# Summing the values of two key tiles in one visit of TensorE, in a transformer layer on one core

## The chip, the cores and the metric

The program runs on one core of one Trainium2 chip, in one launch. The metric is the device time of one execution in microseconds, the median of several runs. A profile of one execution stands beside it, with every instruction's start and length by engine: PE (TensorE), ACT (ScalarE), DVE (VectorE), POOL (GpSimd), and SP, which issues the DMAs.

## The reference

The input is 8 sequences of 1024 tokens of 256 channels, in float32. Four parts follow one another, each added to the running value after a layer norm:

```python
x = x + retention(layernorm(x), ...)     # 4 heads, chunks, gates: "attn_a"
x = x + ffn(layernorm(x), ...)
x = x + attention(layernorm(x), ...)     # 16 heads of 16 channels: "attn_b"
x = x + ffn(layernorm(x), ...)           # the same weights again
```

What the change touches is the attention:

```python
scores = jnp.einsum('bhqd,bhkd->bhqk', q, k) / np.sqrt(HEAD_DIM)
attn = jax.nn.softmax(scores + bias[None], axis=-1)
out = jnp.einsum('bhqk,bhkd->bhqd', attn, v)
```

The bias depends on the distance of key and query alone, and is the same for all distances over 128.

## The kernel before, in words

**One planner for all.** The kernel's functions only record operations, each with a target time. `Plan.issue` then emits them in an order of its own: it keeps a clock by estimated costs, and whenever an engine is free it takes, among the operations of that engine that are ready and whose tiles find a buffer, the one of the smallest key. The key is the target plus surcharges. So the work of several sequences is mixed on each engine: retention and feed-forward parts of later sequences stand between the attention of earlier ones. The emitted order is fixed when the program is built. All instructions bear line 608, that of `emit`; they are told apart by their tiles.

**Modes of TensorE.** `record` gives each matmul operation a mode: `rows` (64 rows of the array, two heads side by side: tiles `p`, `s`, `aps`, and `ops` from the state `S`), `cols` (`sps`), `acc` (four heads side by side in columns: tile `acc`), and `all` (the full array). Matmuls that are recorded in direct succession into the same tile become one operation. In `issue` a change of mode costs `SWITCH` and a surcharge on the key.

**The table of rules.** For every `STRETCH` of 20 us of the planner's clock, one hexadecimal digit of `TURNS` chooses one of 16 `RULES`: the surcharge for a change of mode, how many PSUM tiles must be free for going to `p` or `s`, how many sums must be ready for going to `acc`, and shifts for `p`, `s` and `acc`.

**The attention of one sequence.** `maxima` computes scores by query tile for pairs of heads (`p`, TensorE) and VectorE takes their maxima (`pm`, with `jmax` where the near bias from `hk1` is added). `shift` puts the maxima into the query rows `q`. `weigh` then goes over four groups of four heads and two halves of 512 queries. For each of eight steps `n` it takes, for both pairs `pr` of heads, one tile of 128 keys: TensorE makes transposed scores in two PSUM tiles `s`, and ScalarE writes their exponentials into a tile `e` (tag `e2`, 128 x 2 x 512). Where the bias is near, ScalarE copies that part instead, POOL adds `hk2`, and ScalarE takes the exponential of the part (in the very last group VectorE adds instead). `values(n, es)` sums weighted values of the four heads into `acc`, four matmuls for one step, which the profile shows as eight records. The sums of a step are recorded after the exponentials of the next one:

```python
es.append(e)
if last is not None:
    values(*last)
last = (n, es)
```

So at most four tiles `e` are in use by recorded steps, and `NE` gives six buffers. After the eighth step ScalarE copies `acc` to `o`, and a DMA stores it to `od`. `back` divides by the sums, applies the output weights (`bop`) and runs the second feed-forward part (`kps`, `rps`, `yps`).

PSUM has seven tiles for everything but `acc` (`slots["one"]`); `p` and `s` take two each time.

Of the kernel before, what the change touches and what calls it, by code (L numbers as in the profile page):

```python
# [41 lines left out]
NC, CT = 4, 2 * P  # L42
VW = AHD + 1
NJ = 5
NE = 6

LEAD = 0.3

# [28 lines left out]

STRETCH = 20
TURNS = (
    "00070270877472bf8931ef967bfe1d0522ff04383dfe37be3f1f7ef668e19e9c33271224f3e73df5"  # L80
    "5663e6176b19fd77763fbb3cafd79ff9fb9bf84111"
)
SWITCH = 0.1

# [527 lines left out]
def layer_kernel(ctx: ExitStack, tc: tile.TileContext, ap: dict, out: bass.AP):  # L612
# [20 lines left out]
    def tile2k(tag, bufs=1, dt=F32):  # L633
        return plan.tile([P, HALF], dt, tag, tag, bufs)

    def misc(name):
        return plan.tile([P, HALF], F32, "one", name, 0, "psum")

    def mm(o, lhsT, rhs, start=True, stop=True, share=1.0, group=None):
        n = 1  # L640
        for d in rhs.shape[1:]:
            n *= d
        pe.matmul(o, lhsT, rhs, start=start, stop=stop, group=group,
                  cost=share * (0.004 + (4 if rhs.dtype == F32 else 1) * max(n, 64) / 2400.0))
# [66 lines left out]
    def small(shape, name, bufs=2, dt=F32):  # L711
        return plan.tile(shape, dt, name, name, bufs)
# [522 lines left out]
    def two(ps, q, k, qc, kc, queries):  # L1235

        group = object()
        for hh in range(2):
            r = slice(hh * HROWS, (hh + 1) * HROWS)
            a, m = (k[r, kc], q[r, qc]) if not queries else (q[r, qc], k[r, kc])  # L1240
            mm(ps[hh] if isinstance(ps, list) else ps[:, hh, :], a, m, share=0.525, group=group)

    def near_bias(j, tag, bufs):

        t = plan.tile([P, 2, 2 * P], F32, tag, tag, bufs)
        sp.dma_start(
            t, ud.raw(2 * j * NU, [[1, P], [NU, 2], [1, 2 * P]]),
        )
        return t
# [61 lines left out]
    def weigh(b, g):  # L1311

        plan.target = b + LEAD + (g - 0.5) / NG
        va = plan.tile([P, NT, 4 * VW], F32, "va", "va", 2)
        sp.dma_start(va, vd[b % 2][g].rearrange("n p w -> p n w"))
        hank = [near_bias(2 * g + i, "hk2", 3) for i in range(2)]
        alone = b == B - 1 and g == NG - 1
        for hf in (1, 0):

            def near_of(kt):  # L1320
                return [qr for qr in (NT - 2 - kt, NT - 1 - kt) if qr >= 0 and qr // 4 == hf]


            kts = sorted(range(NT), key=lambda kt: (not near_of(kt), kt))
            far = sum(not near_of(kt) for kt in kts)
            kts = [kt for n in range(NT) for kt in (kts[n : n + 1] + kts[NT - far + n : NT - far + n + 1])]
            kts = list(dict.fromkeys(kts))
            turns = [kts, [kts[n ^ 1] for n in range(NT)]]

            def values(n, es):  # L1330
                for j in range(4):
                    kt = turns[j // 2][n]
                    mm(acc[32 * j : 32 * j + VW, :], va[:, kt, j * VW : (j + 1) * VW],
                       es[j // 2][:, j % 2, :], n == 0, n == NT - 1, share=0.2535)

            last = None
            for n in range(NT):
                es = []
                for pr in range(2):
                    kt = turns[pr][n]  # L1340
                    plan.target = b + LEAD + (4 * NT * g + 2 * NT * (1 - hf) + 2 * n + pr) / (4 * NT * NG)
                    near = near_of(kt)
                    q, k = stacks[b, 2 * g + pr]
                    ps = [misc("s") for _ in range(2)]
                    two(ps, q, k, slice(hf * HALF, (hf + 1) * HALF), slice(kt * P, (kt + 1) * P), False)
                    e = plan.tile([P, 2, HALF], F32, "e2", "e2", NE)
                    if near:
                        c0, c1 = (near[0] % 4) * P, (near[-1] % 4 + 1) * P
                        h0 = (near[0] - (NT - 2 - kt)) * P
                        u = hank[pr][:, :, h0 : h0 + c1 - c0]  # L1350
                        part = e[:, :, c0:c1]
                        for hh in range(2):
                            if alone:
                                dve.tensor_tensor(part[:, hh], ps[hh][:, c0:c1], u[:, hh], ALU.add)
                            else:
                                act.copy(part[:, hh], ps[hh][:, c0:c1])
                            if c0 == P and c1 == 3 * P:
                                cut4 = lambda t: t.rearrange("p (a w) -> p a w", w=P)[:, 0:4:3, :]
                                act.activation(cut4(e[:, hh]), cut4(ps[hh]), AF.Exp)
                            else:  # L1360
                                for a0, a1 in ((0, c0), (c1, HALF)):
                                    if a1 > a0:
                                        act.activation(e[:, hh, a0:a1], ps[hh][:, a0:a1], AF.Exp)
                        if not alone:
                            pool.tensor_tensor(part, part, u, ALU.add)
                        act.activation(part, part, AF.Exp)
                    else:
                        for hh in range(2):
                            act.activation(e[:, hh], ps[hh], AF.Exp)
                    es.append(e)  # L1370
                if last is not None:
                    values(*last)
                last = (n, es)
            values(*last)

            o = tile2k("o")
            act.copy(o[:, ::-1], acc)
            sp.dma_start(od[b][1 - hf, 4 * g : 4 * g + 4].rearrange("h d t -> (h d) t"), o)
            if g == NG - 1:
                sums = small([P, AH * HALF // P], "sums")  # L1380
                sp.dma_start(
                    sums, od[b].raw(((1 - hf) * AH * 32 + AHD) * HALF, [[32 * HALF, AH], [64, 8], [1, 64]])
                )
                dve.reciprocal(sums, sums)
                sp.dma_start(rd[b].raw((1 - hf) * AH * HALF, [[64, P], [1, 64]]), sums)
# [33 lines left out]
    for b in range(B):  # L1419
        retention(b)  # L1420
        if b == 0:
            plan.target = -0.9
            later()
        ffn_front(b)
        project_b(b)
        for j in range(NPAIR):
            maxima(b, j)
            shift(b, j)
        for g in range(NG):
            weigh(b, g)  # L1430
        back(b)
# [21 lines left out]
```

## Time and profile before

| | before |
|---|---|
| median of 3 runs | 2548.52 us (2542.09 to 2551.93) |
| profiled execution | 2557.27 us |
| its span, first to last instruction | 2555.5 us |
| TensorE's matmuls busy | 2476.2 us |
| VectorE busy | 2107.5 us |
| ScalarE busy | 2069.9 us |
| POOL busy | 1589.0 us |
| granted clock of TensorE, mean | 0.992 |
| DMA traffic | 251.17 MB, 98 GB/s |

The page's busy time of an engine is the union of its records, so overlapping instructions count once. Its slices are 40 equal parts of the span, 64 us each, with the busy share in tenths. A line of a group gives the operation, its tiles and shape, the count, the busy time and the mean length of one, and the idle time before them with what ended it. A line of the timeline gives start, length, engine, operation and count; instructions of one kind in a row are merged. A line of the windows view gives a stretch, its length, the busy time of PE, PE's weight loads, DVE, ACT and POOL with the number of instructions, the granted clock, the DMA share and GB/s.

### The profile page before, as it was taken

The page shows a single profiled execution, that of the slowest core. Times are in us where ns is not written, and L with a number is a line of the kernel's source. Part 1 is how long each engine was busy: PE and PEld are TensorE (multiplying, and loading weights), DVE is VectorE, ACT ScalarE, POOL GpSimd, SP SyncE. Part 2 cuts the span into 40 slices and gives each one's busy share as a digit, 9 for nine tenths or more (in the row PEclk, how much of TensorE's full clock was granted, in tenths as well). Part 3 has the DMA queues.
Part 4 walks back from the last instruction along what each step waited for, and adds up shares of the span by engine and source line. Part 5 has one row for each costly group of instructions (what it writes and reads, how often), then busy time and mean ns, then how long its engine had stood idle before and what let it go on. Part 6 is the DMA issues. An engine that isn't in the chain of part 4 may idle for free.

```text
span 2555.5 us, 51508 instructions
## 1 busy us (share of the span) xinstructions
PE 2476.2 (97%) x15814; PEld 1459.8 (57%) x15814; DVE 2107.5 (82%) x6230; ACT 2069.9 (81%) x5334; POOL 1589.0 (62%) x2675
## 2 busy tenths in 40 slices
PE   5999999999999999999999999999999999999997
PEld 3887755555555555555555555555555555554555
DVE  6767998888888888988888788888888888788855
ACT  3565598888989888988888789988898888688883
POOL 2467666666756666666656576666666666666642
PEclk9999999999999999999999999999999999999999
DMA  7136322444344333332324333333233344444322
GB/s 175 42 108 150 81 58 68 130 107 112 85 106 105 84 100 101 110 98 79 92 64 119 97 107 102 94 78 109 68 94 93 102 118 115 124 115 113 93 64 72
DMA packets 252224, 251.17 MB, mean 98 GB/s; under 512 B 89042, under 2 KB 226180, under 8 KB 251924
## 3 DMA queue, kind: packets, MB, share of 16 engines
q1 hardware_dynamic: 251956, 247.89, 36.6%
q8 instruction: 132, 2.16, 0.4%
q14 instruction: 136, 1.11, 0.2%
HBM read 151.32 MB, written 98.59 MB: 98 GB/s over the span
## 4 chain that ended last, share of the span: by engine, by line
PE 79%; DVE 8%; DMA 5%; ACT 3%; POOL 2%; issue 1%; SPq 1%; POOLq 0%; DVEq 0%; ACTq 0%
PE acc L608 16%; PE p L608 10%; PE s L608 10%; PE kps L608 4%; PE wps L608 4%; PE yps L608 4%; PE rps L608 4%; PE qkp L608 3%; PE vps L608 3%; PE qps L608 3%; PE gps L608 3%; PE ops L608 3%; DVE pm L608 3%; ACT e L608 2%; PE bop L608 2%
## 5 line engine op out<-in xcount | busy, mean ns | idle before, releaser
L608 DVE TENSOR_REDUCE pm<-p 128x1 f32<-128x512 f32 (+2 forms) x2048 | 1057.2, 557 | 89.7 <-PE p L608 87.9
L608 ACT ACTIVATE e<-s 128x512 f32<-128x512 f32 (+2 forms) x2048 | 1008.0, 527 | 52.8 <-PE s L608 49.3
L608 POOL TENSOR_TENSOR e<-e,hk 128x512 f32<-128x512 f32 (+1 forms) x558 | 614.0, 1107 | 348.7 <-ACT e L608 326.9
L608 PE MATMUL acc<-e,va 128*17 128x512 f32 x4096 | 529.5, 599 | 3.7 <-ACT e L608 3.4
L608 DVE CUSTOM_DVE_ANT_0 jmax<-p,hk 128x256 bf16<-128x256 f32 (+1 forms) x1152 | 427.0, 371 | 111.8 <-PE p L608 106.6
L608 ACT COPY e<-s 128x256 f32<-128x256 f32 (+1 forms) x1116 | 400.0, 358 | 82.3 <-PE s L608 80.2
L608 PE MATMUL p<-k,q 64*128 64x512 f32 x2048 | 460.4, 438 | 5.0 <-DVE pm L608 2.8
L608 PE MATMUL s<-q,k 64*128 64x512 f32 x2048 | 456.7, 436 | 5.8 <-DVE pm L608 3.2
L608 ACT ACTIVATE e<-e 128x512 f32<-128x512 f32 (+1 forms) x576 | 336.2, 586 | 59.0 <-POOL e L608 56.1
L608 PEld LDWEIGHTS p<-k,q 64*128 64x128 f32 x2048 | 207.5, 185 | 248.4 <-ACT e L608 93.7
L608 PEld LDWEIGHTS s<-q,k 64*128 64x128 f32 x2048 | 206.0, 185 | 204.6 <-issue 69.8
L608 PEld LDWEIGHTS acc<-e,va 128*17 128x17 f32 x4096 | 77.7, 95 | 189.5 <-issue 161.6
L608 PE MATMUL kps<-xk,W_k 128*128 128x256 f32 x512 | 130.8, 399 | 10.7 <-DVE xk L608 9.7
L608 PE MATMUL rps<-W_r,xr 128*128 128x256 f32 x512 | 126.8, 390 | 3.0 <-DVE pm L608 1.8
L608 PE MATMUL yps<-W_v,xk 128*128 128x256 f32 x512 | 127.2, 392 | 1.1 <-DVE pm L608 0.5
L608 PE MATMUL wps<-wo_a,gs 128*128 128x256 f32 x512 | 125.7, 388 | 0.6 <-ACT gs L608 0.5
L608 PEld LDWEIGHTS kps<-xk,W_k 128*128 128x128 f32 x512 | 95.2, 195 | 40.7 <-issue 19.3
L608 PE MATMUL qps<-wqk,nT 128*128 128x512 f32 x384 | 106.8, 413 | 7.0 <-DVE nT L608 6.6
L608 PEld LDWEIGHTS rps<-W_r,xr 128*128 128x128 f32 x512 | 93.4, 191 | 34.5 <-DVE pm L608 5.1
L608 PEld LDWEIGHTS yps<-W_v,xk 128*128 128x128 f32 x512 | 93.6, 192 | 28.7 <-issue 12.0
L608 PEld LDWEIGHTS wps<-wo_a,gs 128*128 128x128 f32 x512 | 92.5, 190 | 26.5 <-issue 4.7
L608 POOL TENSOR_TENSOR ao_y<-ao_a,mhalf 128x4 f32<-128x4 f32 x64 | 65.7, 1026 | 66.5 <-DVE ao_a L608 65.8
(185 smaller groups left out, 4175.3 us busy)
## 6 DMA issues: line engine op xcount, KB each, us to landing
stk<-qk SPq DMA_DIRECT2D x192, 256.0 KB
hk<-ud SPq DMA_DIRECT2D x128, 256.0 KB
q<-stk SPq DMA_DIRECT2D x128, 256.0 KB
k<-stk SPq DMA_DIRECT2D x128, 256.0 KB
od<-o SPq DMA_DIRECT2D x64, 256.0 KB
vd<-vst SPq DMA_DIRECT2D x64, 136.0 KB
va<-vd SPq DMA_DIRECT2D x32, 272.0 KB
xc<-in_x SPq DMA_DIRECT2D x32, 256.0 KB
```

The costliest lines, as they stand in the source:

```text
L608: getattr(real, method)(*[be(a) for a in args], **{k: be(a) for k, a in kw.items()})
```

## The change

The sums of two steps are now recorded in direct succession, at steps 2, 4 and 6 and after the last, and so become one operation of eight matmuls. `NE` rises to seven. `TURNS` is another table; `RULES` stay. No other function changes, but the planner's order changes for nearly the whole program.

```diff
-NE = 6
+NE = 7
...
 TURNS = (
-    "00070270877472bf8931ef967bfe1d0522ff04383dfe37be3f1f7ef668e19e9c33271224f3e73df5"
-    "5663e6176b19fd77763fbb3cafd79ff9fb9bf84111"
+    "000702700732e6dd891a1c0bbe1177118b0437404827e18153eed9e7b7ef1b0fd7ff7e268eb7790c"
+    "edb60a1fee678765e731ce598123a1ab8131b5b918111"
 )
...
-            last = None
+
+            held = []
             for n in range(NT):
                 es = []
...
                     es.append(e)
-                if last is not None:
-                    values(*last)
-                last = (n, es)
-            values(*last)
+                held.append((n, es))
+                if n % 2 == 0 and n > 0:
+                    values(*held.pop(0))
+                    values(*held.pop(0))
+            while held:
+                values(*held.pop(0))
```

## The prediction, made before the changed kernel ran

> **What bounds the kernel now.** The first page line read is the busy time by engine, then the slices, then the chain.
>
> ```profile
> PE 2476.2 (97%) x15814; PEld 1459.8 (57%) x15814; DVE 2107.5 (82%) x6230; ACT 2069.9 (81%) x5334; POOL 1589.0 (62%) x2675
> PE   5999999999999999999999999999999999999997
> ACT  3565598888989888988888789988898888688883
> PE 79%; DVE 8%; DMA 5%; ACT 3%; POOL 2%; issue 1%; SPq 1%; POOLq 0%; DVEq 0%; ACTq 0%
> ```
>
> TensorE is full in every slice but the first and the last, and 79% of the chain is its own work. ScalarE and VectorE have about a fifth of their time to spare, in every slice, the last quarter included. So what counts is how long TensorE's list of instructions takes, and after that whether some stretch asks more of ScalarE or VectorE than of TensorE. The groups show who feeds whom:
>
> ```profile
> L608 DVE TENSOR_REDUCE pm<-p 128x1 f32<-128x512 f32 (+2 forms) x2048 | 1057.2, 557 | 89.7 <-PE p L608 87.9
> L608 ACT ACTIVATE e<-s 128x512 f32<-128x512 f32 (+2 forms) x2048 | 1008.0, 527 | 52.8 <-PE s L608 49.3
> L608 PE MATMUL acc<-e,va 128*17 128x512 f32 x4096 | 529.5, 599 | 3.7 <-ACT e L608 3.4
> ```
>
> The busy time of a group doesn't price a matmul, since records overlap. The timeline of TensorE does, from one start to the next:
>
> ```profile
> 1403.43 0.39 PE L608 MATMUL p<-k,q 64*128 64x512 f32 x2
> 1403.67 0.39 PE L608 MATMUL s<-q,k 64*128 64x512 f32 x2
> 1403.99 1.05 PE L608 MATMUL acc<-e,va 128*17 128x512 f32 x8
> 1404.97 0.50 PE L608 MATMUL p<-k,q 64*128 64x512 f32 x2
> ...
> 1420.70 1.91 PE L608 MATMUL acc<-e,va 128*17 128x512 f32 x16
> 1422.54 0.53 PE L608 MATMUL p<-k,q 64*128 64x512 f32 x2
> 1422.88 0.42 PE L608 MATMUL s<-q,k 64*128 64x512 f32 x2
> 1423.11 0.41 PE L608 MATMUL p<-k,q 64*128 64x512 f32 x2
> ```
>
> One tile's sums alone take 0.98 us (1403.99 to 1404.97), two tiles' together 1.84 (1420.70 to 1422.54): a visit costs 0.12 on top of 0.86 a tile. A pair of half-row matmuls (p or s) takes 0.24 in the middle of a visit (1403.43 to 1403.67), 0.34 as the first after a switch (1422.54 to 1422.88) and 0.32 as the last before one (1403.67 to 1403.99): a visit costs 0.20 there. Medians over the whole trace say the same (0.983, 1.841, 0.232, 0.336, 0.327). The full-array products of eight records take 1.92 between two switches and 1.73 between none: 0.20 again.
>
> **Term 1: fewer visits, -26 us.** The order of the built programs gives the counts. TensorE visits the sums 429 times before (346 single, 83 double) and 256 times after, all double: 173 x 0.125 = 21.6 us less. Visits to half-row work (p, s, aps, ops from S) fall from 873 to 812: 61 x 0.20 = 12.2 less. Visits to full-array work rise from 576 to 597, and transposes end more of them, whose leaving costs 0.17: 7 to 8 more. Column-split visits (sps) stay at 55. In all TensorE's list, priced so, falls from 2408 to 2382 us: -26. Of the span of 2555.5 before, about 148 are thus not list but start, end and waits.
>
> **Term 2: waits of the sums in the body, -10 us.** A tile with a near block needs ACT's copies and exponentials, POOL's addition and a last exponential: from the end of its s matmuls to its last write the median is 3.4 us, against 1.6 for a far tile. In the waits view the sums wait for this 35 times:
>
> ```profile
> PEld acc L608 <- ACT e L608: 16.1, 35, 2.5
> ```
>
> What covers the wait is TensorE's work between s and sums. In the first 2140 us of its list, 31 of 445 tiles' sums have under 3.4 us of cover for a near tile before, 1 of 422 after, since a pair waits longer and the seventh buffer lets s run on. I take 10 of the 16.1 away; bounds are all 16 gone, and 10 more instead of fewer, because a pair now waits for four tiles at once, and behind it in TensorE's order stand the s and p that ScalarE and VectorE live on. The seventh buffer itself adds no instruction. DMAs are the same in number, and SP's rows move with their users; ACT's copy of the sums and the store od<-o follow the last sums as before. I cost those at nothing, being covered by 97% busy TensorE; uncovered, the longest such step on the chain was 8.8 us (od<-o).
>
> **Term 3: the end of the kernel, +53 us.** Holding four tiles for each pair slows s, so the body takes more full-array work per p and s, and this runs out early. In TensorE's own work, the last sequence's 128 pairs of p stand in 171 us after (2151 to 2322), in 247 before; its 128 pairs of s in 154 us (2197 to 2351), in 222 before. But a p pair costs VectorE 1.27 us from start to start (reductions 0.47 each, jmax 0.34 or 0.21), and an s pair costs ScalarE 1.26 on average (exponentials 0.48 for 512 columns, 0.28 for 256; copy 0.25; last exponential 0.53). Pricing both engines' instructions that stand beside each 20 us of TensorE's list, from 2140 to 2360, I get for ScalarE 18, 24, 24, 21, 17, 19, 15, 25, 25, 30, 20 and for VectorE 21, 23, 22, 24, 18, 17, 14, 25, 25, 12, 15. The larger of the two, where it is over 20, exceeds TensorE by 34 us in sum; the old order exceeds by 1 in this stretch, and by 7 in the body, where the new one exceeds by 1. Two humps are thus bound by ScalarE and VectorE together.
>
> How full an engine gets when it binds is the unknown. The nearest rows are old stretches that are rich in s:
>
> ```profile
> 2440.00:2460.00 20.00, 19.84 (x115) 10.82 (x114) 13.61 (x41) 16.41 (x43) 14.25 (x21) 1.00 0.24 75
> 2460.00:2480.00 20.00, 20.00 (x124) 10.09 (x126) 8.36 (x26) 18.81 (x45) 5.64 (x14) 1.00 0.15 47
> 2480.00:2500.00 20.00, 19.71 (x124) 9.85 (x116) 9.97 (x28) 17.90 (x43) 7.48 (x16) 1.00 0.24 70
> ```
>
> The fourth number after the length is ScalarE: 82 to 94% busy. The seven pieces that clearly bind hold 174 us of work; at 94% they take 11 more, at 82% 38 more, at 90% 19 more. I take 90%, since seven PSUM tiles hold only three pairs and each double sum shuts TensorE to s and p for 1.84 us. So 34 + 19 = 53. The top is 72. The bottom is 26: three pairs in flight at 1.27 us carry about 4 us over each hump's edge, twice.
>
> **Sum.** -26 - 10 + 53 = +17 us. The profiled execution took 2557.27 us, 2555.5 of it span, 0.3% over the median of 2548.52; the difference is put on the median: 2565.5. A difference of 0.5%, 12.7 us, is about what a measurement of this kernel can tell from no change.
>
> **The clock, row and rule.** The granted clock, third from the end, is 1.00 in the rows above, but in these it is not:
>
> ```profile
> 1425.00:1437.00 12.00, 10.65 (x70) 5.98 (x66) 7.94 (x25) 7.96 (x22) 6.82 (x14) 1.00 0.54 125
> 1437.00:1445.00 8.00, 7.89 (x25) 5.18 (x25) 4.17 (x12) 4.11 (x11) 3.04 (x5) 0.57 0.13 37
> ```
>
> TensorE was busy for 10.65 of 12 us, and then ran at 0.57. Short waits in a row can thus halve it here for some 7 us, at up to 3.4 us each. The Trainium skill, "TensorE: Matmul & The Clock Gate" (A second HAM failure mode: psum-queue depth-cycling) speaks against the change more strongly: a TensorE that idles briefly between groups while PSUM buffers cycle swings between half and full clock. By that rule the humps would be half-clocked again and again and the sum would be the second rival's; by the row, one or two drops, which the range holds.
>
> **Rivals.** First, on the other side: the end's overload is absorbed. The place is the two humps; the price is their 34 us less what buffers and a reordering of arrivals take off. Below 23 us there, the visits saved win by over 0.5%: with 18 it is -26 - 10 + 18 = -18, 2530. For it speaks that ScalarE and VectorE run behind TensorE by whole tiles already and that only 34 are forced; against it that the order is fixed when the program is built, so that the slack between the humps (17, 19, 15 of 20) can't be used for work of a later hump. Chance 0.16.
>
> Second, the humps also halve the clock: one drop of 6.8 us in each of the eight pieces over 20, at 3.4 each, +27, 2592. For it speaks the 0.57; against it that even a hump leaves TensorE about 75% busy. Chance 0.10.
>
> Third, a draw: the end costs 24 to 48 us and the visits pay for it, around 2550. Chance 0.27. That the sums are not taken together after all is no rival: all 256 visits in the order are double.
>
> The forecast itself, the end at 49 to 72 us without more drops, has 0.47. So faster by over 0.5% is 0.16, within 0.5% 0.27, slower 0.47 + 0.10 = 0.57. The range takes term 2 at its better bound and the end at its bottom: -26 - 16 + 26 = -16, 2533; and term 2 at its worse bound and the end at its top: -26 + 10 + 72 = +56, 2604. It holds most of the first rival and the second's 2592.
>
> **What would show it.** In the changed profile the sums stand only as x16 in TensorE's timeline; the sums' wait for e outside the last 300 us is nearly gone; TensorE's slices fall to 8 or 7 between about 2260 and 2530 us, where ScalarE's rise to 9. Term 1 is wrong if double sums take more than 1.84 us from start to start or the first p and s after a switch more than 0.34; term 3 is wrong if TensorE stays at 9 to the end, or if its waits there name DMAs and not e and pm.

## The result and the profile after

| | before | after |
|---|---|---|
| median | 2549.97 us (4 runs, 2542.09 to 2551.93) | 2593.46 us (4 runs, 2590.02 to 2596.8) |
| profiled execution | 2557.27 us | 2591.02 us |
| its span | 2555.5 us | 2589.3 us |
| granted clock of TensorE, mean | 0.992 | 0.993 |

The ratio is 1.0172, with a 95% interval of 1.0159 to 1.0186: slower by 43.5 us of the medians, by 33.8 us in the two profiled executions. The profiled execution of before was 7.3 us above its median, that of after 2.4 below. No profile can tell where these 10 us come from, so what the traces explain is a step of 34 us. The mean granted clock is the same in both, so the clock as a whole is not the loss.

The page of after, busy time, slices and chain:

```profile
PE 2499.1 (97%) x15814; PEld 1490.8 (58%) x15814; DVE 2111.0 (82%) x6230; ACT 2069.3 (80%) x5334; POOL 1592.9 (62%) x2675
PE   5999999999999999999999999999999999999997
ACT  3564589888888888888888888888888788888893
PE 77%; DVE 11%; ACT 5%; DMA 2%; POOL 2%; issue 2%; SPq 0%; DVEq 0%; POOLq 0%; ACTq 0%
```

TensorE's slices stay at 9 to the end, so the page seems to say that nothing is lost. It misleads: a record lasts longer than its place in the pipeline (0.39 us and more for a pair of `p` or `s`, whose place is 0.23), so TensorE is busy by its records where it is held up. The group of the sums, after, shows this (operation, tiles and shape, count; busy time, mean of one; idle time before, and what ended it):

```profile
L608 PE MATMUL acc<-e,va 128*17 128x512 f32 x4096 | 498.7, 603 | 0.7 <-ACT e L608 0.7
```

The sums take 31 us less of busy time (529.5 before, 498.7 after), since the records of a double visit overlap, and hardly wait for `e` (3.4 before, 0.7 after). What has grown is the waiting of the engines that read scores, here the waits of before and after (us, times, longest):

```profile
ACT e L608 <- PE s L608: 129.4, 178, 10.4
DVE jmax L608 <- PE p L608: 106.6, 157, 2.7
```

```profile
ACT e L608 <- PE s L608: 144.2, 205, 2.6
DVE jmax L608 <- PE p L608: 131.8, 157, 2.8
```

ScalarE and VectorE wait 40 us more for TensorE's scores, although TensorE has less to do. To see where, I priced every operation of TensorE from its start to the next start, as the prediction did (0.983 a single sum, 1.841 a double one, 0.232 a pair of `p` or `s`, and so on). What an interval holds beyond its price is called a wait below (a stretch of lower clock counts in it too). Before, the waits add up to 124 us, after, to 184. In span time, the waits from 2250 us on are 27 before and 91 after, and those ahead of it 97 and 93. Of the 64 us more, some 57 stand before the last sums begin (at 2502.4 us before, 2531.9 after), and 8 behind that. So the sum is -26 for the list, -4, +57 and +8, which is +35 against 33.8 measured.

Windows of the stretch from 2250 us on, first after, then before (rows picked from the view; length; PE, weight loads, DVE, ACT, POOL with their instructions; granted clock; DMA share; GB/s):

```profile
2280.00:2300.00 20.00, 19.27 (x101) 7.79 (x101) 16.45 (x50) 16.37 (x43) 8.54 (x7) 0.91 0.71 186
2300.00:2320.00 20.00, 19.37 (x100) 7.93 (x98) 16.74 (x56) 16.41 (x47) 5.61 (x7) 0.91 0.09 30
2440.00:2460.00 20.00, 18.22 (x104) 7.92 (x104) 16.99 (x58) 17.87 (x52) 9.01 (x8) 1.00 0.46 122
2480.00:2500.00 20.00, 17.92 (x99) 6.30 (x93) 9.41 (x29) 16.83 (x50) 8.30 (x8) 0.92 0.08 16
```

```profile
2280.00:2300.00 20.00, 20.00 (x124) 10.71 (x123) 19.01 (x58) 18.30 (x48) 12.29 (x19) 1.00 0.24 70
2300.00:2320.00 20.00, 19.83 (x126) 9.75 (x118) 18.09 (x54) 15.99 (x41) 11.36 (x20) 1.00 0.27 81
```

Here the number of matmuls tells more than the busy time: 101 and 100 after, 124 and 126 before. A part of this is the clock, 0.91 in these two windows, but from 2440 to 2460 us it is 104 at a clock of 1.00. ScalarE and VectorE aren't full either (16.4 and 16.5 of 20 in the first row). All three engines wait for one another. The timeline of TensorE after, from 2446 us, shows how:

```profile
2446.12 0.50 PE L608 MATMUL p<-k,q 64*128 64x512 f32 x2
2446.45 0.40 PE L608 MATMUL s<-q,k 64*128 64x512 f32 x2
2446.68 0.39 PE L608 MATMUL p<-k,q 64*128 64x512 f32 x2
2446.91 0.98 PE L608 MATMUL s<-q,k 64*128 64x512 f32 x2
2447.59 0.90 PE L608 MATMUL p<-k,q 64*128 64x512 f32 x2
2449.51 0.76 PE L608 MATMUL s<-q,k 64*128 64x512 f32 x2 [1.02 <-ACT e L608]
```

Three pairs follow one another at 0.33 and 0.23 us. The fourth begins on the seventh tile and waits for an eighth: 0.68 us to the next start. The fifth takes 1.92, until ScalarE has read an `s`. I call a series of `p` and `s` pairs a run if neither sums nor other TensorE work of at least 0.8 us breaks it. Before, 13 runs are longer than three pairs, after, 65, and 31 of these have five to eleven pairs. Among the pairs from 2250 us on that follow another pair directly, 114 stand fourth or later in a run. Their intervals hold 49 us of waits, and those of the third pairs just ahead of them another 5: some 55 us, 0.5 for each further pair. This is nearly all of the 57. Second and third pairs otherwise wait 0.0 and 0.1. In the sums below, the waits of a run from its third pair on are counted in this way.

### The profile page after: what moved, and what is told of

It reads as the page before. It is cut to its first block, busy times and chain, and to the rows that moved or that the text cites. A ratio compares the mean times of both kernels' runs of the same rounds, so it can differ in the third digit from the quotient of the medians.

```text
span 2589.3 us, 51539 instructions
## 1 busy us (share of the span) xinstructions
PE 2499.1 (97%) x15814; PEld 1490.8 (58%) x15814; DVE 2111.0 (82%) x6230; ACT 2069.3 (80%) x5334; POOL 1592.9 (62%) x2675
## 4 chain that ended last, share of the span: by engine, by line
PE 77%; DVE 11%; ACT 5%; DMA 2%; POOL 2%; issue 2%; SPq 0%; DVEq 0%; POOLq 0%; ACTq 0%
PE acc L608 15%; PE p L608 10%; PE s L608 9%; DVE pm L608 5%; PE kps L608 4%; PE wps L608 4%; PE yps L608 4%; PE rps L608 4%; PE qps L608 3%; ACT e L608 3%; PE gps L608 3%; PE qkp L608 3%; PE vps L608 3%; PE ops L608 3%; PE bop L608 2%
## 5 line engine op out<-in xcount | busy, mean ns | idle before, releaser
L608 PE MATMUL acc<-e,va 128*17 128x512 f32 x4096 | 498.7, 603 | 0.7 <-ACT e L608 0.7
L608 PE MATMUL s<-q,k 64*128 64x512 f32 x2048 | 480.5, 435 | 10.0 <-ACT e L608 2.1
L608 PE MATMUL p<-k,q 64*128 64x512 f32 x2048 | 480.1, 443 | 6.8 <-DVE pm L608 2.5
L608 PEld LDWEIGHTS s<-q,k 64*128 64x128 f32 x2048 | 219.8, 185 | 196.8 <-issue 67.7
L608 PEld LDWEIGHTS acc<-e,va 128*17 128x17 f32 x4096 | 95.4, 97 | 239.3 <-issue 232.1
```

The source lines that it names most:

```text
L608: getattr(real, method)(*[be(a) for a in args], **{k: be(a) for k, a in kw.items()})
```

## The experiments

Theories first. A: the loss is in the new order's end, where ScalarE and VectorE get too much at once. B: joining itself costs, in any order. C, formed after the first four runs: a joined sum costs where it leaves more than three pairs in a run, because PSUM holds three. D and E, then F and G, stand with their runs.

**All sums joined in the old order.** The old table plans; afterwards each sum is held back to the next one.

```diff
+        for op, news in self.made:
+            if op.mode == "acc" and held is None:
+                held = op, news
+                continue
```

> The old program's order, planned with single sums and the old table, and only then joined: each first sum of two waits in the order until the second one, or until the seven buffers are used up. Everything else keeps its place. TensorE visits the sums 262 times instead of 429, all switches fall from 1933 to 1672, and the feed-forward work stays where it was (13 of the last chunks' bop in TensorE's last 240 us of list, 15 before, 8 in the changed kernel). Theory A (pairs are cheap in themselves; the loss is that the new order has used up its full-array work before the end): the list, at 2408 us before, is 2370, so 39 us less, and waits grow by no more than 10: 2510 to 2525. Theory B (a double sum costs waits in itself, since it needs four tiles and shuts TensorE to p and s for 1.84 us): no better than before, 2550 to 2590.

Measured: 2680.56 us, ratio 1.0502 (1.0486 to 1.0518). Both theories missed by far. The list is 38 us shorter than before, yet the waits are 284 us instead of 124. Pairs that stand fourth or later in a run number some 270 (counted as above), and with them go some 140 us of waits, of the 160 more. The timeline (TensorE, with those rows of its weight loads and of ScalarE that bear on it; other rows are left out):

```profile
1509.88 0.50 PE L645 MATMUL s<-q,k 64*128 64x512 f32 x2
1510.22 0.39 PE L645 MATMUL p<-k,q 64*128 64x512 f32 x2
1510.42 1.08 ACT L645 ACTIVATE e<-s 128x512 f32<-128x512 f32 x2 [1.96 <-PE s L645]
1510.46 0.39 PE L645 MATMUL s<-q,k 64*128 64x512 f32 x2
1510.69 0.87 PE L645 MATMUL p<-k,q 64*128 64x512 f32 x2
1511.07 0.18 PEld L645 LDWEIGHTS p<-k,q 64*128 64x128 f32 x1 [0.42 <-ACT e L645]
1511.56 0.28 PEld L645 LDWEIGHTS s<-q,k 64*128 64x128 f32 x2 [0.31 <-ACT e L645]
1511.56 0.59 PE L645 MATMUL s<-q,k 64*128 64x512 f32 x2
1512.11 0.66 PE L645 MATMUL p<-k,q 64*128 64x512 f32 x2
```

The granted clock was 1.00 from 1509 to 1514 us. Three pairs pass at 0.34, 0.24 and 0.23 us, then ScalarE's exponentials give the pace, 0.87 and 0.55. And ScalarE itself stood 1.96 us before the first `s`: first it starves, then it is what TensorE waits for.

**The new order with every double sum split.** After planning, the first four matmuls of a double sum move up to where their `e` is ready.

```diff
+            if op.mode != "acc" or len(op.calls) != 8:
+                continue
...
+            where.setdefault(pe[i], []).append((half[0], news))
+            where.setdefault(n, []).append((half[1], []))
```

> The changed program's order, but each double sum is split after the planning, its first half put earlier, at the first place in TensorE's order at which the planner's own clock had its tiles ready. 511 visits instead of 256, list 2444 us instead of 2383; the end stays overloaded (26 us by prices, 34 in the changed kernel). Theory A: slower than the changed kernel by most of the 61 us of list, 2635 to 2655. Theory B: the waits of the double sums go and pay for the visits, 2590 or less.

Measured: 2668.63 us, 1.0456 (1.0440 to 1.0471), 14 above A's bound and far from B. There are 511 visits to the sums instead of 256, and the list grows from 2382 to 2444 us: 0.24 a visit, the 0.125 for the sums and the switches to half-row work around it. Waits are 198 us, 184 with double sums. In the order that was planned for them, the double sums bring no more waits than single ones, so B falls there. The run is 76 us longer in the profile, 62 of it list.

**The end with short exponentials and maxima, new order and old.** In the last sequence the whole-tile ones work on 128 of 512 columns. This kernel leaves out three quarters of those scores, and the sums read the 128 columns four times over, so TensorE's work stays.

```diff
+            if op.light:
+                args = [a[:, :128] if isinstance(a, View) and a.shape == [P, HALF] else a for a in args]
```

> The changed program's order, but in the last sequence the exponentials and the maxima of whole 512-column tiles take 128 columns alone (112 of each; the sums read those 128 four times). That takes some 36 us from ScalarE and 45 from VectorE, nothing from TensorE's list. Theory A: the 50 us of waits in the last sequence were those engines' overload, so 30 to 45 us are gained: 2550 to 2565. Theory B: the waits come from the visits, at most 15 are gained: 2578 or more.

> The control: the same lightening of the last sequence in the old program's order. Theory A: ScalarE and VectorE did not bind there, at most 8 us are gained: 2542 to 2550. If the lightening is worth 30 us here too, e3 says nothing of an overload by the new order.

Measured: 2584.08 us, 1.0121 (1.0106 to 1.0137) in the new order, and 2549.45, 0.9986 (0.9976 to 0.9996) in the old one. ScalarE's busy time fell by 33 us (2069.3 to 2036.2) and VectorE's by 38 (2111.0 to 2072.8), all of it in the last sequence, and the time by 9 (13 by the ratios; the control in the old order gained some 4). A wanted 30 to 45, B at most 15. So the end is bound at most in small part by how much these two engines have to do, and A falls in this form. The waits from 2250 us on fell only from 91 to about 81.

**Sums joined only up to three, or up to four, pairs in a run.** As the first experiment, with a look ahead:

```diff
-            if op.mode == "acc" and held is None:
+            if op.mode == "acc" and held is None and joins(op) <= MOST:
```

> The old order, and a first sum waits for the second only where no more than three pairs of p and s then follow one another between sums or long full-array work: 370 visits of the sums instead of 429 (262 in e1), list 2401 us instead of 2408, and 18 pairs stand behind the third of their run, as before (317 in e1). Theory C, formed from e1 and e3: seven PSUM tiles hold three pairs, each further pair of a run waits about 0.6 us, and joining costs only where it makes such runs: 7 us less than before, 2538 to 2550. Theory B (joining costs in itself; e1 lost 128 us with 167 visits fewer, 0.77 us for each): 59 x 0.77 = 45 us more, 2585 to 2605.

> As e5, with up to four pairs in a run: 330 visits, list 2389 us, 69 pairs behind the third instead of 18. Theory C: 20 us less list, 51 x 0.56 = 28 us more waits: 8 more than before, 2552 to 2568. Theory B: 99 x 0.77 = 76 us more, 2615 to 2640.

Measured: 2582.16 us, 1.0127 (1.0112 to 1.0142), with 370 visits and 18 pairs beyond the third, as many as before; and 2612.78, 1.0249 (1.0232 to 1.0266), with 330 visits and 69 such pairs. C fails the first: 59 joins cost 32 us (22 between the profiled executions) where no run grows beyond three. Between the two runs C's wait is there (42 fourth pairs at 0.76 us, 32 in sum), on top of something else. B's forecasts lie only 3 and 2 us above the two results, so in this fixed order B isn't refuted. The 30 us of waits more in the first are spread over many tiles, no one above 7 (`rps` 6.5, `mxp` 4, `acc` 1.6). But they share a place: some 22 of the 30 lie between the start of a third pair and the start of work that is neither a pair nor sums (16 us before, 38 here). That work takes its tiles from the same seven, so C may have drawn its line one pair too late. No run tests this.

**Only the end split.** The second experiment, for double sums after 2150 us of the planner's clock:

```diff
-            if op.mode != "acc" or len(op.calls) != 8:
+            if op.mode != "acc" or len(op.calls) != 8 or now < 2150:
```

> The changed program's order with its double sums up to about 2150 us of the planner's clock, and split as in e2 from there on: 301 visits instead of 256, list 2396 instead of 2383, and 64 pairs behind the third of their run in the last 240 us of list instead of 122. Theory C: 13 us more list, 58 x 0.56 = 32 us less waits, some 20 us faster than the changed kernel: 2566 to 2582. Theory A as an overload of ScalarE and VectorE: the waits stay, 13 us slower than the changed kernel: 2600 to 2612.

Measured: 2595.25 us, 1.0176 (1.0159 to 1.0193). The list is 14 us longer, the waits are 176 instead of 184 us. Both forecasts missed (C 2566 to 2582, A 2600 to 2612): splitting pays for itself in the end, no more. From 2250 us on the pairs beyond the third fell from 114 to 59 and the waits that go with them from 55 to 32, but the waits of the sums and of what follows a third pair grew by some 12. So breaking up the runs moved half of their waits elsewhere. I read this as a stretch that has little but scores and sums left to do; it isn't shown.

**One rule for the whole program, old code and new.** Rule number 5 of `RULES`, counted from 0, in place of either table.

```diff
-TURNS = (...)
+TURNS = ("5")
```

> The old code with one rule (number 5) for the whole program in place of the found table: list 2425 us, 414 visits, 39 pairs behind the third of their run. Base for e9. Theory C: 17 us more list and 21 x 0.56 = 12 us more waits than before, and whatever the table spared at the end: 2575 to 2640.

> The changed code with one rule (the fifth) for the whole program in place of its found table; to be compared with the code before under the same rule (2605.85 us). Its list is 44 us shorter than that one's, but 309 pairs of p and s stand behind the third of a run. If it is the joined sums that cost, whatever the table: 90 to 110 us above 2605.85. If the loss was the poorer luck of the new table: no more than 2606.

Measured: 2605.85 us, 1.0218 (1.0203 to 1.0234) for the old code, and 2742.89, 1.0753 (1.0729 to 1.0777) for the new: 137 us more, above the forecast of 90 to 110, and with the other sign from a theory of an unlucky table. Pairs beyond the third are 26 with some 11 us of waits in the old code, 280 with some 140 in the new, 0.5 each. The found table of after avoids most of these. So under this one rule the new table is no cause of the loss but what keeps it small; other rules were not tried.

**Short exponentials and maxima in every sequence.** Again the kernels leave out three quarters of the scores of whole tiles. Theory D: the waits that joining brings are the time in which ScalarE and VectorE read. Theory E: they are latencies of other kinds.

```diff
-                            plan.ops[-1].light = b == B - 1
+                            plan.ops[-1].light = True
```

> The order before, in every sequence the whole-tile exponentials and maxima read 128 of 512 columns (the sums then read these 128 four times over), so ScalarE and VectorE have some 25 to 30% less to do; TensorE's list stays at 2408 us. It is the control for the next two runs. Both theories: 2515 to 2548 us, since only the waits of p, s and sums (some 44 of 124 us) can go.

> The same shorter exponentials and maxima, in the order before with all sums joined after planning (the list is 38 us shorter than the control's). Theory D: the waits that joining brought (160 us more than before in the run with all sums joined) are ScalarE's and VectorE's reading time against three pairs in PSUM; with shorter reads at most 50 are left, and the time is between 38 us below and 12 us above the control. Theory E: they are fixed latencies (semaphores, POOL's additions, copies) in an order that was planned tight for single sums; 100 or more are left, and the time is 60 us or more above the control.

> The same shorter exponentials and maxima, with sums joined only where no more than three pairs of p and s then follow one another (list 7 us shorter than the control's). At full length this joining cost 32 us. Theory D: no more than 3 us above the control. Theory E: 18 us or more above it.

Measured: control 2527.37 us, 0.9907 (0.9888 to 0.9926); all joined 2621.53, 1.0274 (1.0257 to 1.0291), 94 above it; joined up to three 2544.34, 0.9970 (0.9957 to 0.9983), 17 above it. At full length these were 128 and 32, each against before in its own series. E holds for the first (60 or more); the second lies just under its bound of 18, and D (at most 12 and 3) fails in both. Shorter reading takes a quarter off the cost of joining, and half where only 59 are joined. With pairs beyond the third still go 0.4 us each, some 114 us in sum instead of 140. A reason can be read from the trace: from the start of its matmul to the end of its last read a tile of `p` is in use for 1.93 us and one of `s` for 1.75 (medians, all sums joined), and with short reads for 1.41 and 1.53. The read itself is less than half of that. The rest must be the way from TensorE to the reader, and the wait behind what else stands in its queue; these two weren't told apart.

**ScalarE's copy of the sums moved.** In the run with all sums joined ScalarE stood 66.6 us before its copy `o`, 16.6 before. Theory F: this holds up the exponentials behind it, and so the PSUM tiles. Theory G: it costs nothing by itself.

```diff
+            if op.eng == "ACT" and any(t.tag == "acc" for t in op.tiles):
+                late.append((op, news))
...
+                if passed[0] == LATER:
+                    flush()
```

> The order before, no sums joined, but ScalarE's copy of the sums (o) and its store stand three ScalarE operations later, and e has seven buffers. It is the control for the next two runs, and shows the seventh buffer by itself. Both theories: 2542 to 2556 us.

> All sums joined in the old order, as in the run of 2680.56 us, but ScalarE's copy of the sums stands three ScalarE operations later. Theory F: a joined last sum comes later, ScalarE stands before its copy (66.6 us in that run against 16.6 before) with the exponentials behind it in its queue, and these hold the PSUM tiles; at most 2655 us. Theory G: ScalarE would have had nothing else to do in that time; 2672 us or more.

> Sums joined up to three pairs, as in the run of 2582.16 us, but with ScalarE's copy three operations later (its wait was 28.6 us there, 16.6 before). Theory F: 2565 to 2574 us. Theory G: 2578 us or more.

Measured: control 2568.94 us, 1.0057 (1.0036 to 1.0078); all joined 2675.53, 1.0479 (1.0460 to 1.0498); joined up to three 2600.56, 1.0187 (1.0167 to 1.0206). The control missed its range: with no sum joined, 64 copies three places later, together with seven buffers for `e`, cost 15 us. Its waits point to the copy:

```profile
PEld acc L688 <- ACT o L688: 29.2, 32, 1.4
PE acc L688 <- ACT o L688: 18.3, 28, 0.9
```

There is one `acc`, and now the next group's first sum waits for the copy (4.6 and 0.2 us before). The weight loads and the matmuls wait at the same time, so this is 29 us in all. By their numbers G holds in both runs. Against the control joining up to three costs 32 us as it did without the move (F falls there), and joining all costs 107 instead of 128. So the copy is at most 21 us of those 128, and moving it only shifts the wait to TensorE. The control has seven buffers too, so these 32 us don't come from the seventh buffer.

**What is settled and what isn't.** Settled is that double sums in the order planned for them bring no more waits than single ones; that some 0.4 to 0.8 us of waits go with each fourth and later pair in a run; that such waits, and not the two engines' amount of work, go with the large losses (some 140 of 160 us more in the first experiment, and in the one with one rule); and that they are 55 us in the end of after. That three pairs of PSUM tiles cause them is read from the timelines and from the seven tiles; no run changes that number, and the split end shows that shorter runs alone don't win the time back. That the runs there come from full-array work that was used up earlier is read from the order (in the last 240 us of the list 15 operations of `bop` stand before, 8 after), not shown by a run. Open is the 32 us of 59 joins in a fixed order. Some 22 of their 30 us of waits follow a third pair, and the control with moved copies shows that even a small displacement costs this order 15 us; a single cause was not shown. No version here that computes the whole result beats the kernel before.

## Why the prediction was right or wrong

Its direction was right and the time lies in its range, but the loss was forecast at 17 us over the median, and is 43.5 (34 in the profiled pair). The step that failed is term 3's price: the end was charged with the work of ScalarE and VectorE in excess of TensorE's, and what the runs show there is TensorE waiting in long runs of pairs. Two more terms were mis-sized: the body's waits (-10 forecast, -4 measured) and the chain behind the last sums (nothing forecast, +8 measured). With what was measured the sum is -26 - 4 + 57 + 8 = +35. Step by step:

**Term 1, fewer visits, -26: right.** In the timeline of after the sums stand only as x16, for example:

```profile
1402.71 1.91 PE L608 MATMUL acc<-e,va 128*17 128x512 f32 x16
1411.51 1.91 PE L608 MATMUL acc<-e,va 128*17 128x512 f32 x16
```

The prices held, and the run with every sum split fits from the other side (62 us of list more, 76 of time).

**Term 2, waits in the body, -10: mis-sized.** The sums' waits for `e` are nearly gone, as forecast (their weight loads waited 16.1 us for it before, 3.4 after), but the waits up to 2250 us in all fell by 4. Even these 4 are the clock's: up to 2250 us the clock's drops cost some 17 us before and 7 after. So other work waits for what the sums no longer wait for: I took one line of the waits view as a saving, though the engine behind it stays as it is. This is 6 of the missing us.

**Term 3, the end, +53: size near, mechanism wrong.** From 2250 us to the last sums the waits grew by 57 us. I had the 53 from the work of ScalarE and VectorE in excess of TensorE's, with both 90% busy. But cutting the reading of whole tiles there to a quarter gave back only some 9 us, only one of ScalarE's slices there (2460 to 2525 us) rose to 9, and its windows of 20 us from 2240 to 2520 hold 15.3 to 19.8. Some 55 of the 57 stand in runs of more than three pairs. The step that failed is the choice of the overload as price; that 53 came near 57 is luck. The sentence on seven PSUM tiles, which only served to pick 90%, named what the timelines point to. What I named as a sign, TensorE's slices at 8 or 7, didn't come: by the prediction's own words that would make term 3 wrong. It was a bad sign rather, since busy records hide such waits; the starts of matmuls against their prices are a better one.

**The very end: not in the sum.** After the last sums, the last sequence's back part runs almost alone. From their start to the end of the span it takes 53.1 us before and 57.4 after, although TensorE's list there is some 3 us shorter. In the timeline of TensorE after:

```profile
2535.67 1.99 PE L608 MATMUL bop<-wo_b,ob 128*128 128x256 f32 x8
2541.80 3.38 PE L608 MATMUL bop<-wo_b,ob 128*128 128x256 f32 x8 [4.14 <-DVE ob L608]
2545.02 0.60 PE L608 MATMUL ftp<-cm,z 128*128 128x128 f32 x4
2547.70 0.83 PE L608 MATMUL kps<-xk,W_k 128*128 128x256 f32 x2 [2.09 <-DVE xk L608]
```

Before, more other full-array work lay between these steps. This gave 8 us of waits. I had seen that full-array work runs out early, and priced what that does to `p` and `s`, but not to the chain that ends last.

**The median.** I put the difference of a profiled pair on the median. The profiled execution of before lay above all its timed runs, and so 10 us of the medians' difference stand outside any trace.

**The clock.** Drops came: from 2240 us on four windows of 20 us at 0.91 or 0.92, and one at 0.83 (2540 to 2560); the double sum at 2289.10 took 3.37 us. From 2250 us to the last sums the granted clock is 1.00 before and 0.98 after, which is 7 of the 57 us. Over the whole span the body's fewer drops make up for it (0.992 and 0.993). The Trainium skill, "TensorE: Matmul & The Clock Gate" (A second HAM failure mode: psum-queue depth-cycling), describes for another kernel the situation that the runs show, a TensorE that stalls in turn with its PSUM buffers. What it says of the clock itself didn't follow to that extent: in the timeline above from 2446 us the stalls come one after another with the granted clock at 1.00. The second rival's 2592 is near the result, but not for its reason: it wanted eight halved pieces of 6.8 us, 27 us in all (its own rows name seven pieces over 20).

**A reading.** That ScalarE has a fifth of its time to spare in every slice was too kind: the slices shown there have it at 9 in 7 of 40.

## What to carry to other kernels

Count how many results of TensorE can wait at once in PSUM, and look in the new order for places where more than that many producers follow one another: here each further one went with waits of 0.4 to 0.8 us, a part of the buffer's whole round trip of some 1.9, and still with 0.4 where its readers had much less to read. A switch saved is worth its price only if what stood between the visits finds another place. Judge a stretch by the starts of operations against list prices, not by the busy share.

## What was unexpected of the hardware

A TensorE that is 97% busy by its records held 184 us of waits in 2589. And moving one copy in 64 groups by three places in ScalarE's order, with no work added and one buffer more for `e`, cost 15 us; TensorE's sums then waited 29 us for the copy, where they had waited under 5.
